# Expert gates applied to the tokens instead of to the expert outputs, in a windowed-attention and mixture-of-experts block

## The chip, the cores and the metric

The kernel runs on one core of a Trainium2 chip. The core has five engines that run side by side, each with its own queue of instructions: TensorE (PE in the profile; its weight loads are listed as PEld), VectorE (DVE), ScalarE (ACT), GpSimd (POOL) and SyncE (SP), which here only starts transfers. An engine works through its queue in order; where an instruction needs a result of another engine it waits, and what is queued behind it waits too. TensorE writes its results to PSUM, which this kernel uses as eight banks of 128 x 512 float32; the other operands lie in SBUF. The metric is the time of one execution on the device in microseconds, the median of several runs; the profile is of one execution.

## What is computed

The input x is 2 x 128 x 256 x 256 (batch, channels, rows, columns), float32. One layer follows: a channel normalisation and attention in windows of 8 x 8 pixels with a fixed mask that leaves only every second row and column, and on top of the sum with x a second normalisation and eight experts, of which each pixel takes the two best.

```python
x = x + _L0_conv_ref(_ln_c(x), W_qkv, W_out, rel_height, rel_width)   # window attention
t = _to_tokens(x)                                                     # one token per pixel, 128 channels
t = t + _L0_ffn_ref(_ln_t(t), router_w, router_b, expert_w, expert_b)
x = _from_tokens(t, x)

def _L0_ffn_ref(x, router_w, router_b, expert_w, expert_b):
    router_probs = jax.nn.softmax(x @ router_w + router_b, axis=-1)
    top_p, top_i = jax.lax.top_k(router_probs, K)                     # K = 2 of E = 8
    top_p = top_p / jnp.sum(top_p, axis=-1, keepdims=True)
    expert_out = jnp.einsum('bnd,edc->bnec', x, expert_w) + expert_b
    gathered = jnp.take_along_axis(expert_out, top_i[..., None], axis=2)
    return jnp.einsum('bnk,bnkc->bnc', top_p, gathered)
```

For each pixel the layer is thus the sum over the experts of gate times (normalised token times expert matrix, plus bias), where six of the eight gates are zero.

## The kernel before

**Tiling.** The image is cut into 64 strips of eight rows (32 for each batch element). A strip is one tile `xt` of 128 channels x 8 x 256, 1 MB, of which six fit (`xpool`). Because the mask couples only pixels of the same parity of row and column, the attention of a strip is done in four planes, n = 4i + pl, each of 4 x 128 = 512 pixels. The main loop runs over the 256 planes and six more steps that drain what is left. In a step n = 4i + pl four things are under way: the attention of plane n (`scores`, `attend`, `out_project`), the projection of the plane after it (`project`), the router for two rows (512 tokens) of the strip before (`norms`, `route`, with f = (i-1, pl)), and the experts for the rows routed one step earlier (`experts`). The same step also normalises two rows of the next strip for the attention (`norms` with c, then `ln1_c`).

**Normalisation.** `stats` transposes 512 tokens on PE (L211, tiles `px_f` and `px_c`) so that a token's channels lie along a row, and DVE takes their statistics (L213). `rstd` makes 1/std from them in ten small steps (L222 to L231). The means need no subtracting, since the weights were centred beforehand. `ln1_c` needs 1/std of each pixel on all 128 channel partitions: PE transposes a broadcast of it (L262, tile `pb`) and DVE multiplies (L265) into `xn`.

**Attention.** `project` makes q (L279, copied by ACT at L281), the relative position terms (`pu`, L288, followed by DVE's L290, L295 twice and L300), the keys (`pk`, L312, copied by ACT at L319), POOL's gather of the columns (L305) and the values (`pvv`, L329, copied at L336). `scores` adds up the scores in PSUM by many small matmuls (L357 and 128 of L372, two records each) and takes the exponential on ACT (L380). `attend` multiplies with the values (L391, L399), and DVE divides (L409 to L418). `out_project` multiplies with the output matrix (L424) and DVE adds into `xt` (L428).

**Router.** `norms` multiplies the tokens with the router matrix (L444, tile `plt`; copied by ACT at L452). `route` transposes the logits back to tokens on partitions (L466, `plg`), and a chain of DVE steps with one exponential on ACT (L470 to L496) finds the two best and leaves the gates in `gate` and the gates times 1/std in `gx`, with tokens on partitions.

**Experts.** `experts` transposes the gates (L505, `pg`) for a bias matmul (L511, `pbias`, copied to `acc` at L514). Then, for each 128 tokens, two matmuls of 128 x 512 (L520) apply four experts each, with the tokens as the stationary operand, so that the results have tokens on partitions and a gate is one number for each partition. DVE takes four experts from PSUM, multiplies by the gate and adds to `acc` (L531); ACT multiplies the other four by theirs (L535) into `others`, which POOL adds up (L536, L539, L540). At the end PE transposes `acc` back to channels (L544, `py`) and DVE adds it into `xt` (L545). After the fourth pair of rows the strip is stored (L552). `experts` is a generator: the main loop calls it in pieces with `next(parts)`, and finishes it as `behind` in the step after.

**Order.** The framework's scheduler sets the order on each engine, with the program's order as priority and a model of durations: what is ready earlier in its model can be put ahead of what is written earlier. It also makes the semaphores. PSUM has four rotating banks for matmul results (`ps_mm`) and four for the attention scores (`ps_att`). SP carries only the 1 MB loads (L98) and stores (L552) of the strips once the program has begun.

Of the kernel before, what the change touches and what calls it, by code (L numbers as in the profile page):

```python
# [16 lines left out]
P = 128  # L17
HEADS, DH = 4, 32
E = 8
SCALE = DH ** -0.5  # L20
CONV_EPS, FFN_EPS = 1e-6, 1e-5
NEG = -1e30

# [19 lines left out]
def kernel(  # L43
# [33 lines left out]
    ps_mm = ctx.enter_context(tc.tile_pool(name="ps_mm", bufs=4, space=PSUM))  # L77
# [72 lines left out]

    eb = ctile([NT * E, NT, P], "eb")
    nc.vector.memset(eb, 0.0)
    for t in range(NT):
        nc.scalar.dma_start(eb[t * E : (t + 1) * E, t, :], expert_b)
# [60 lines left out]
    def rstd(st, eps, n, name):  # L215

        u = small.tile([P, 2 * NT], F32, tag="u", name=f"u_{name}")[:, 0:n]
        d = small.tile([P, 2 * NT], F32, tag="d", name=f"d_{name}")[:, 0:n]  # L220
        r = small.tile([P, 2 * NT], F32, tag="r", name=f"r_{name}", bufs=6)[:, 0:n]
# [9 lines left out]
        nc.vector.scalar_tensor_tensor(r, u, 3.0, r, ALU.add, ALU.mult)  # L231
        return r
# [25 lines left out]
    def ln1_c(i, k, rs):  # L258

        pb = mm_tile(f"pb{i}_{k}")  # L260
        for t in range(NT):
            nc.tensor.transpose(  # L262
                pb[:, t * P : (t + 1) * P], rs[:, t : t + 1].broadcast_to([P, P]), ident
            )
        nc.vector.tensor_tensor(  # L265
            xn[i % 2][:, :, :, k, 1 : PC + 1],
            ln1_src(i, k).rearrange("p (y j x) -> p y x j", y=2, x=2),
            pb.rearrange("p (y j x) -> p y x j", y=2, x=2),
            ALU.mult,
        )  # L270

    def project(n, state):
# [12 lines left out]


        pu = mm_tile(f"pu{n}")
        nc.tensor.matmul(pu, lhsT=wrel, rhs=inner, start=True, stop=True)  # L288
        uT = work.tile([P, PR, 4, 32], F32, tag="uT", name=f"uT{n}")
        nc.vector.transpose(uT, pu.rearrange("p (a m s) -> p a s m", a=PR, s=4))  # L290
        for j in range(2):
            shifted = uT[:, :, :, NU * j + 3 : NU * j + 9]
            dims = [list(d) for d in shifted.ap]
            dims[1 + j][0] -= 1
            nc.vector.tensor_copy(  # L295
                auT[n % 2][:, :, :, 6 * j : 6 * j + 6],
                bass.AP(shifted.tensor, shifted.offset, dims),
            )
        au = work.tile([P, 2 * NP, PR, 4], F32, tag="au", name=f"au{n}")
        nc.vector.transpose(au.rearrange("p m a s -> p a s m"), auT[n % 2])  # L300
# [23 lines left out]

        vv = work.tile([P, HP, P], F32, tag="vv", name=f"vv{n}")
# [11 lines left out]
        state.update(qs=qs, kk=kk, au=au, vv=vv)  # L337
        yield
# [8 lines left out]
    def scores(n, state):  # L347

# [17 lines left out]
        for t in range(HP):  # L366
            for half in range(2):
# [13 lines left out]
        state.update(att=att, pT=pT)  # L381

# [47 lines left out]
    def norms(f, c, nm):  # L430


        st = small.tile([P, 2 * NT, 6], F32, tag="st", name=f"st{nm}", bufs=4)
        n0, n1 = (0 if f else NT), (2 * NT if c else NT)
        lT = None
# [17 lines left out]
        if not (f or c):  # L453
            return None, None, None
        r = rstd(st[:, n0:], epsc[:, n0:n1], n1 - n0, nm)
        return (r[:, 0:NT] if f else None), (r[:, NT - n0 :] if c else None), lT
# [4 lines left out]
    def route(i, k, rs, lT):  # L461
# [32 lines left out]
        nc.vector.tensor_tensor(gate, gate, sm.broadcast_to(by_e), ALU.mult)  # L494
        gx = small.tile([P, NT, E], F32, tag="gx", name=f"gx{nm}")
        nc.vector.tensor_tensor(gx, gate, rs.broadcast_to(by_e), ALU.mult)  # L496
        return gate, gx

    def experts(i, k, gate, gx):


        nm = f"{i}_{k}"
        src = rows_of(i, k)
        pg = mm_tile(f"pg{nm}")
        nc.tensor.transpose(pg[: NT * E, :P], gate.rearrange("p t e -> p (t e)"), ident)  # L505
        gT = small.tile([NT * E, P], F32, tag="gT", name=f"gT{nm}")
        nc.scalar.copy(gT, pg[: NT * E, :P])
        yield
        acc = work.tile([P, NT, P], F32, tag="acc", name=f"acc{nm}")
        pb = mm_tile(f"pbias{nm}")  # L510
        nc.tensor.matmul(  # L511
            pb, lhsT=gT, rhs=eb.rearrange("r t c -> r (t c)"), start=True, stop=True
        )
        nc.scalar.copy(acc.rearrange("p t c -> p (t c)"), pb)  # L514
        yield
        for t in range(NT):
            others = work.tile([P, 4, P], F32, tag="others", name=f"others{nm}_{t}")
            for e0 in range(0, E, 4):
                pe = mm_tile(f"pe{nm}_{t}_{e0}")
                nc.tensor.matmul(  # L520
                    pe,
                    lhsT=src[:, t * P : (t + 1) * P],
                    rhs=ew[:, e0 : e0 + 4, :].rearrange("p e c -> p (e c)"),
                    start=True,
                    stop=True,
                )
                for e in range(e0, e0 + 4):
                    pe_e = pe[:, (e - e0) * P : (e - e0 + 1) * P]
                    g = gx[:, t, e : e + 1]
                    if e < 4:  # L530
                        nc.vector.scalar_tensor_tensor(  # L531
                            acc[:, t, :], pe_e, g, acc[:, t, :], ALU.mult, ALU.add
                        )
                    else:
                        nc.scalar.activation(others[:, e - 4, :], pe_e, AF.Copy, scale=g)  # L535
            nc.gpsimd.tensor_tensor(  # L536
                others[:, 0:2, :], others[:, 0:2, :], others[:, 2:4, :], ALU.add
            )
            nc.gpsimd.tensor_tensor(acc[:, t, :], acc[:, t, :], others[:, 0, :], ALU.add)  # L539
            nc.gpsimd.tensor_tensor(acc[:, t, :], acc[:, t, :], others[:, 1, :], ALU.add)  # L540
            yield
        py = mm_tile(f"py{nm}")
        for t in range(NT):
            nc.tensor.transpose(py[:, t * P : (t + 1) * P], acc[:, t, :], ident)  # L544
        nc.vector.tensor_add(src, py, src)  # L545
        if k == R // 2 - 1:
            store(i)
        yield
# [6 lines left out]

    halo(0)
    for k in ln_rows(0):
        ln1_c(0, k, norms(None, (0, k), f"_{k}")[1])
    n_planes = 4 * len(strips)
# [4 lines left out]
    parts, behind = none, none  # L564
    for n in range(n_planes + 6):
        i, pl = divmod(n, 4)
        live = n < n_planes
        if pl == 0:
            load_x(i + 3)
            if i + 1 < len(strips):  # L570
                halo(i + 1)
        next(parts, None)
        if live:
            scores(n, states[n])
        f = (i - 1, pl) if 0 < i <= len(strips) else None
        rows = list(ln_rows(i + 1))[-4:] if i + 1 < len(strips) else []
        ks = [k for k in rows if (k - 2) % 4 == pl or (k == 1 and pl == 0)]
        if i + 1 < len(strips) and strips[i + 1][1] == 0:
            ks = list(ln_rows(i + 1))[pl::4]
# [83 lines left out]
```

## Time and profile before

| | |
|---|---|
| three runs | 5860.81 us median, 5839.03 to 5871.58 |
| the profiled execution | 5851.49 us, of which the span from its first to its last instruction is 5849.7 us |
| granted TensorE clock over the span | 0.974 |
| L531, DVE | 4096 instructions, 1394.6 us, 340 ns each |
| L535, ACT | 4096 instructions, 1199.5 us, 369 ns each |
| L536, L539, L540, POOL | 1024 each, 758.3, 479.0 and 468.1 us |
| L520, PE | 4096 records, two for a matmul; 184.0 us of idle time before them, put down to L535 |
| loads and stores | 64 each of 1024 KB, 4.8 and 5.2 us from issue to landing |
| HBM traffic | 23 GB/s over the span |

A group's line in the profile names its source line, engine and operation, the tile written and the tiles read, the shape, and how many there were; then come busy time, mean duration, and the time for which the engine sat idle just before, with what ended it. In an order of time the first figure is the start in us from the beginning of the span, the second the duration; a bracket gives idle time before the instruction and what released it. Durations of matmuls include their way through the array, so that consecutive ones overlap: the time that a matmul takes away from TensorE is read from start to start. A float32 matmul leaves two records.

### The profile page before, as it was taken

How to read it: one execution, taken by the hardware profiler on the slowest of the kernel's cores; microseconds unless marked ns; L12 is line 12 of the kernel's file. 1: busy time of each engine (PE TensorE's matmuls, PEld its weight loads, DVE VectorE, ACT ScalarE, POOL GpSimd, SP SyncE). 2: the span in 40 equal slices, each digit the busy share in tenths (PEclk: the TensorE clock that was granted, in tenths of full speed). 3: DMA queues.
4: the chain of work that ended last, by engine and by line, in shares of the span. 5: the costliest groups of instructions: out<-in, count | busy, mean ns of one | idle time of the engine just before them, and what ended most of it. 6: DMA issues, size and time to landing. Idle time of an engine off the chain costs nothing.

```text
span 5849.7 us, 221084 instructions
## 1 busy us (share of the span) xinstructions
PE 5470.1 (94%) x95758; PEld 3226.5 (55%) x95758; DVE 4262.2 (73%) x14184; ACT 2504.6 (43%) x7189; POOL 2057.8 (35%) x3667
## 2 busy tenths in 40 slices
PE   6999999999999999999999999999999999999998
PEld 4555555555555555555555555555555555555554
DVE  4767777767767777767767777767767767767766
ACT  2434444444444444444444444444444434434444
POOL 1333333333333333333333333333333333333334
PEclk8999999999999999999999999999999999999998
DMA  1000000000000000000000000000000000000000
GB/s 51 17 31 17 31 24 23 31 17 31 31 17 31 31 17 31 31 17 31 17 31 31 17 31 28 20 31 17 31 31 17 31 24 24 31 17 31 17 9 23
DMA packets 21957, 149.32 MB, mean 26 GB/s; under 512 B 2906, under 2 KB 4602, under 8 KB 4602
## 3 DMA queue, kind: packets, MB, share of 16 engines
q1 hardware_dynamic: 18432, 134.23, 6.1%
q8 instruction: 755, 12.37, 0.9%
q14 instruction: 216, 1.77, 0.1%
q10 hardware_dynamic: 2554, 0.95, 0.1%
HBM read 68.06 MB, written 67.11 MB: 23 GB/s over the span
## 4 chain that ended last, share of the span: by engine, by line
PE 83%; DVE 8%; ACT 6%; issue 2%; DMA 0%; ACTq 0%; POOL 0%; POOLq 0%; DVEq 0%
PE pe L520 32%; PE pvv L329 7%; PE att L372 6%; ACT others L535 6%; PE att L399 5%; PE pbias L511 5%; PE pk L312 4%; PE pq L279 3%; PE pu L288 3%; PE po L424 3%; PE att L357 3%; PE px_f L211 3%; PE att L391 3%; PE py L544 2%; PE px_c L211 2%
## 5 line engine op out<-in xcount | busy, mean ns | idle before, releaser
L520 PE MATMUL pe<-ew,xt 128*128 128x512 f32 x4096 | 2071.4, 629 | 184.0 <-ACT others L535 184.0
L535 ACT ACTIVATE others<-pe,gx 128x128 f32<-128x128 f32 x4096 | 1199.5, 369 | 1874.0 <-PE pe L520 1869.3
L536 POOL TENSOR_TENSOR others<-others 128x256 f32<-128x256 f32 x1024 | 758.3, 741 | 3324.8 <-ACT others L535 3226.3
L531 DVE SCALAR_TENSOR_TENSOR acc<-pe,gx,acc 128x128 f32<-128x128 f32 x4096 | 1394.6, 340 | 339.6 <-PE pe L520 301.3
L520 PEld LDWEIGHTS pe<-ew,xt 128*128 128x128 f32 x4096 | 725.8, 193 | 1123.1 <-issue 542.0
L213 DVE BATCH_NORM_STATS2 st<-px_f 128x6 f32<-128x128 f32 x1024 | 228.3, 286 | 959.8 <-PE px_f L211 959.8
L539 POOL TENSOR_TENSOR acc<-acc,others 128x128 f32<-128x128 f32 x1024 | 479.0, 468 | 262.8 <-DVE acc L531 207.1
L329 PEld LDWEIGHTS pvv<-wt,xcol 128*128 128x128 f32 x4096 | 476.9, 191 | 154.3 <-ACT others L535 114.6
L329 PE MATMUL pvv<-wt,xcol 128*128 128x128 f32 x4096 | 522.8, 281 | 1.7
L540 POOL TENSOR_TENSOR acc<-acc,others 128x128 f32<-128x128 f32 x1024 | 468.1, 457 | 75.6
L372 PE MATMUL att<-qs,kcol 32*64 32x32 f32 x32768 | 404.7, 225 | 68.5 <-issue 68.2
L380 ACT ACTIVATE pT<-att 128x1024 f32<-128x1024 f32 x256 | 262.3, 1025 | 445.1 <-PE att L372 445.1
L372 PEld LDWEIGHTS att<-qs,kcol 32*64 32x64 f32 x32768 | 396.0, 130 | 74.1 <-issue 73.5
L312 PE MATMUL pk<-xn,wt 128*128 128x390 f32 x1024 | 378.0, 491 | 0.0
L399 PEld LDWEIGHTS att<-pT,vv 64*32 64x32 f32 x32768 | 351.6, 105 | 47.5 <-issue 9.9
L336 ACT COPY vv<-pvv 128x512 f32<-128x512 f32 x512 | 300.8, 587 | 165.5 <-PE pvv L329 165.5
L399 PE MATMUL att<-pT,vv 64*32 64x32 f32 x32768 | 348.8, 201 | 5.5 <-issue 5.0
L305 POOL COPY xcol<-xn 128x480 f32<-128x480 f32 x512 | 302.1, 613 | 120.5 <-DVE xn L265 76.4
L511 PE MATMUL pbias<-eb,gT 32*128 32x512 f32 x512 | 311.7, 690 | 2.8 <-ACT lT L452 2.1
L312 PEld LDWEIGHTS pk<-xn,wt 128*128 128x128 f32 x1024 | 195.6, 191 | 194.9 <-issue 91.6
L424 PE MATMUL po<-o,wt 128*128 128x512 f32 x512 | 264.9, 599 | 12.8 <-DVE o L418 12.8
L300 DVE STREAM_TRANSPOSE au<-auT 128x512 f32<-128x512 f32 x256 | 270.5, 1057 | 0.2
(3777 smaller groups left out, 7019.7 us busy)
## 6 DMA issues: line engine op xcount, KB each, us to landing
xt<-in_x_dram SPq DMA_DIRECT2D x64, 1024.0 KB, 4.8
out_dram<-xt SPq DMA_DIRECT2D x64, 1024.0 KB, 5.2
ew<-in_L_ffn_expert_w_dram ACTq DMA_DIRECT2D x1, 512.0 KB
wall<-in_L_conv_W_qkv_dram ACTq DMA_DIRECT2D x1, 192.0 KB
keys<-in_c_keys_dram ACTq DMA_DIRECT2D x1, 64.0 KB, 7.5
wall<-in_L_conv_W_out_dram ACTq DMA_DIRECT2D x1, 64.0 KB
eb<-in_L_ffn_expert_b_dram ACTq DMA_DIRECT2D x4, 4.0 KB
ties<-in_c_ties_dram ACTq DMA_DIRECT2D x1, 32.0 KB
```

What stands on the lines that cost most here:

```text
L312: nc.tensor.matmul(pk[:, :nk], lhsT=wk, rhs=xp[:, r : r + 3, :].rearrange("p r c -> p (r c)"), start=True, stop=True,)
L329: nc.tensor.matmul(pv[:, t * P : (t + 1) * P], lhsT=xl[:, t0 + t].rearrange("p a k -> p (a k)"), rhs=wv, start=True, stop=True,)
L372: nc.tensor.matmul(sc[rows, h, 32 * t : 32 * t + 32], lhsT=kk[hp, half * HP + t, :], rhs=qs[hp, m0 : m0 + 2].rearrange("p m a s -> p (m a ...
L399: nc.tensor.matmul(av[hp, half, 32 * t : 32 * t + 32], lhsT=vv[rows, t, hp], rhs=pT[rows, h, 32 * t : 32 * t + 32], start=True, stop=True,)
L424: nc.tensor.matmul(po, lhsT=wo, rhs=state["o"].rearrange("p f z -> p (f z)"), start=True, stop=True)
L511: nc.tensor.matmul(pb, lhsT=gT, rhs=eb.rearrange("r t c -> r (t c)"), start=True, stop=True)
L520: nc.tensor.matmul(pe, lhsT=src[:, t * P : (t + 1) * P], rhs=ew[:, e0 : e0 + 4, :].rearrange("p e c -> p (e c)"), start=True, stop=True,)
L531: nc.vector.scalar_tensor_tensor(acc[:, t, :], pe_e, g, acc[:, t, :], ALU.mult, ALU.add)
L535: nc.scalar.activation(others[:, e - 4, :], pe_e, AF.Copy, scale=g)
L536: nc.gpsimd.tensor_tensor(others[:, 0:2, :], others[:, 0:2, :], others[:, 2:4, :], ALU.add)
L539: nc.gpsimd.tensor_tensor(acc[:, t, :], acc[:, t, :], others[:, 0, :], ALU.add)
L540: nc.gpsimd.tensor_tensor(acc[:, t, :], acc[:, t, :], others[:, 1, :], ALU.add)
```

## The change

The gates are applied to the tokens before the expert matmuls. `experts` now multiplies the 512 tokens, channels on partitions, by the gates of one expert (`xe`; every fourth expert on POOL, the others on DVE) and multiplies the product by that expert's matrix as the stationary operand. All eight, and a bias matmul over the eight rows of `ge`, sum in one PSUM bank of their own (`ps_acc`); DVE adds the bank into `xt`. The transposes `py` and the operations L531, L535, L536, L539, L540 and L514 are gone.

For this the gates must lie on all partitions. `route` writes the gates (g0) and the gates times 1/std (g1) into one tile `g`, into which `norms` writes the 1/std of the rows for the attention. `spread` transposes `g` on PE, copies it on ACT, writes it to DRAM, and reads it back with the last nine rows broadcast to all partitions (`gb`, 128 x 9 x 512) and the plain gates as eight rows (`ge`): three transfers on SP in each step. `ln1` takes 1/std from `gb` a step later and runs on POOL; `ln1_now` keeps the way over PE for rows that have no time for this. Rows for the attention are prepared two planes ahead (`rows_at`), and `halo` is called earlier for that.

The main loop is written anew, and within it PE keeps the written order, while the scheduler still orders the other engines. The scores are written in two parts with the q matmul between them; the `pu` group comes after the routing, and the values are made in two pieces after `out_project`. `ps_mm` has three banks for four.

```diff
-    ps_mm = ctx.enter_context(tc.tile_pool(name="ps_mm", bufs=4, space=PSUM))
+    gates = ctx.enter_context(tc.tile_pool(name="gates", bufs=2))
+    dram = ctx.enter_context(tc.tile_pool(name="dram", bufs=3, space=bass.MemoryType.DRAM))
+    ps_mm = ctx.enter_context(tc.tile_pool(name="ps_mm", bufs=3, space=PSUM))
+    ps_acc = ctx.enter_context(tc.tile_pool(name="ps_acc", bufs=1, space=PSUM))
...
+    def ln1(i, k, rb, eng):
+
+        eng.tensor_tensor(
+            xn[i % 2][:, :, :, k, 1 : PC + 1],
+            ln1_src(i, k).rearrange("p (y j x) -> p y x j", y=2, x=2),
+            rb.rearrange("p (y j x) -> p y x j", y=2, x=2),
+            ALU.mult,
+        )
...
         for t in range(HP):
+            if t == HP // 2:
+                yield
             for half in range(2):
...
+        g0, g1 = (
+            g[:, j * NT * E : (j + 1) * NT * E].rearrange("p (e t) -> p t e", t=NT)
+            for j in range(2)
+        )
+        nc.vector.tensor_tensor(g0, gate, sm.broadcast_to(by_e), ALU.mult)
+        nc.vector.tensor_tensor(g1, g0, rs.broadcast_to(by_e), ALU.mult)
+
+    def spread(f, c, g, nm):
+
+
+        lo, hi = (0 if f else 2 * NT * E), (2 * NT * E + NT if c else 2 * NT * E)
+        pg = mm_tile(f"pg{nm}")
+        nc.tensor.transpose(pg[: hi - lo, :P], g[:, lo:hi], ident)
+        gT = small.tile([(2 * E + 1) * NT, P], F32, tag="gT", name=f"gT{nm}")
+        nc.scalar.copy(gT[: hi - lo], pg[: hi - lo, :P])
+        gd = dram.tile([(2 * E + 1) * NT, P], F32, tag="gd", name=f"gd{nm}")
+        nc.sync.dma_start(gd[lo:hi], gT[: hi - lo])
+        gb = gates.tile([P, E + 1, NT * P], F32, tag="gb", name=f"gb{nm}")
+        lo = max(lo, NT * E)
+        nc.sync.dma_start(
+            gb[:, (lo - NT * E) // NT : (hi - NT * E) // NT].rearrange("p e k -> p (e k)"),
+            gd[lo:hi].rearrange("r k -> (r k)").partition_broadcast(P),
+        )
+        ge = None
+        if f:
+            ge = small.tile([E, NT * P], F32, tag="ge", name=f"ge{nm}")
+            nc.sync.dma_start(ge, gd[0 : NT * E].rearrange("(e t) k -> e (t k)", t=NT))
+        return gb, ge
+
+    def experts(i, k, gb, ge):
...
+        acc = ps_acc.tile([P, NT * P], F32, tag="acc", name=f"acc{nm}")
+        for e in range(E):
+            xe = work.tile([P, NT * P], F32, tag="xe", name=f"xe{nm}_{e}", bufs=4)
+            eng = nc.gpsimd if e % 4 == 3 else nc.vector
+            eng.tensor_tensor(xe, src, gb[:, e], ALU.mult)
+            nc.tensor.matmul(acc, lhsT=ew[:, e, :], rhs=xe, start=(e == 0), stop=False)
             yield
-        py = mm_tile(f"py{nm}")
-        for t in range(NT):
-            nc.tensor.transpose(py[:, t * P : (t + 1) * P], acc[:, t, :], ident)
-        nc.vector.tensor_add(src, py, src)
+        nc.tensor.matmul(acc, lhsT=eb, rhs=ge, start=False, stop=True)
+        nc.vector.tensor_add(src, acc, src)
         if k == R // 2 - 1:
             store(i)
         yield
...
+    with tc.manual_schedule(engines={mybir.EngineType.PE}):
+        for n in range(n_planes + 6):
+            i, pl = divmod(n, 4)
+            live = n < n_planes
+            if pl == 0:
+                load_x(i + 3)
+            score = scores(n, states[n]) if live else none
+            ahead = none
+            if n + 1 < n_planes:
+                states[n + 1] = {}
+                ahead = project(n + 1, states[n + 1])
+            next(score, None)
+            next(ahead, None)
+            next(score, None)
+            next(ahead, None)
+            if pl == 3 and i + 2 < len(strips):
+                halo(i + 2)
+            next(parts, None)
+            f = (i - 1, pl) if 0 < i <= len(strips) else None
+            cs = rows_at(n)
+            c = cs[0] if cs else None
+            if f or c:
+                g, rs, lT = norms(f, c, f"_{n}")
+            if spreads and spreads[1]:
+                ln1(*spreads[1], spreads[2][0][:, E], nc.gpsimd)
+            next(parts, None)
+            if live:
+                attend(n, states[n])
+            for _ in parts:
+                pass
+            if f:
+                route(*f, g, rs, lT)
+            next(ahead, None)
+            if spreads and spreads[0]:
+                parts = experts(*spreads[0], *spreads[2])
+            next(parts, None)
+            for c1 in cs[1:]:
+                ln1_now(*c1)
+            next(parts, None)
+            spreads = (f, c, spread(f, c, g, f"_{n}")) if f or c else None
+            if live:
+                out_project(n, states.pop(n))
+            next(parts, None)
+            next(ahead, None)
+            next(parts, None)
+            next(ahead, None)
```

## The prediction

> **What bounds the kernel now.** I read the page's totals first, then the chain that ended last, then the instructions in order of time in one plane of the middle, then the stretches with their granted clock. The page:
>
> ```profile
> span 5849.7 us, 221084 instructions
> PE 5470.1 (94%) x95758; PEld 3226.5 (55%) x95758; DVE 4262.2 (73%) x14184; ACT 2504.6 (43%) x7189; POOL 2057.8 (35%) x3667
> PE 83%; DVE 8%; ACT 6%; issue 2%; DMA 0%; ACTq 0%; POOL 0%; POOLq 0%; DVEq 0%
> PE pe L520 32%; PE pvv L329 7%; PE att L372 6%; ACT others L535 6%; PE att L399 5%; PE pbias L511 5%; PE pk L312 4%; PE pq L279 3%; PE pu L288 3%; PE po L424 3%; PE att L357 3%; PE px_f L211 3%; PE att L391 3%; PE py L544 2%; PE px_c L211 2%
> ```
>
> TensorE sets the end, and the expert matmuls (L520) are a third of it. Lines of PE in order of time (start, duration) in one plane, n = 45:
>
> ```profile
> 1022.10 1.98 PE L520 MATMUL pe<-ew,xt 128*128 128x512 f32 x4
> 1024.03 0.60 PE L262 MATMUL pb<-ident,r__44_15104 128*128 128x128 f32 x4
> 1025.38 1.98 PE L520 MATMUL pe<-ew,xt 128*128 128x512 f32 x4 [0.75 <-ACT others L535]
> 1027.20 1.02 PE L424 MATMUL po<-o,wt 128*128 128x512 f32 x2
> 1028.06 1.02 PE L279 MATMUL pq<-xn,wt 128*128 128x512 f32 x2
> 1038.37 1.12 PE L511 MATMUL pbias<-eb,gT 32*128 32x512 f32 x2
> 1041.24 0.60 PE L544 MATMUL py<-ident,acc 128*128 128x128 f32 x4
> 1043.49 1.12 PE L520 MATMUL pe<-ew,xt 128*128 128x512 f32 x2
> ```
>
> From 1022.10 to the same matmul at 1043.49 a plane takes 21.39 us, of which PE idles 0.75, waiting for ScalarE's L535. A 512-wide matmul occupies PE 0.86 us (po to pq; two records). From start to start the plane is: pe 7.17 in four groups, plg 0.11, pb 0.60, idle 0.75, po 0.86, pq 0.86, pu 0.87, pk 1.46, pvv 1.88, pg 0.21, scores 0.48 and 1.46, px_f 0.49, px_c 0.53, plt 0.36, pbias 1.05, py 0.53, attend 0.46 and 1.26: 21.39.
>
> **What PE loses.** pb (0.60) and py (0.53) go, and the idle 0.75 with L535. Eight expert matmuls stay 512 wide: 8 x 0.86 = 6.88 for 7.17; the bias one 0.86 for 1.05. The gate transpose stays (0.21). 21.39 - 0.60 - 0.53 - 0.75 - 0.29 - 0.19 = 19.03 us a plane. Some 254 planes' worth of FFN work (256, less the shorter ends): 254 x 2.36 = 600 us, a floor of 5250 if nothing new waits.
>
> **The other engines**, per plane (page busy / 256). DVE 16.65: less sixteen L531 (5.45) and L265 (0.68), plus six multiplications of 512 at the 0.68 of L265 and L428 (4.08) and one small operation more (0.16): 14.8. ACT 9.8: less sixteen L535 (4.69) and the L514 copy (0.59): 4.5. POOL 8.0: less L536, L539, L540 (6.66), plus two expert multiplications and the L265 one; 128 elements take 0.46 and 256 take 0.74, so 512 come to about 1.30 (estimate from these rows): 5.3. None passes PE. DMA: the broadcast writes 9 x 512 x 4 B x 128 = 2.36 MB a plane, 4.5 times today's 134 MB in all; the stretch 3028 to 3030 moved 389 GB/s, so 6.1 us of each plane. PSUM tiles fall from four to three: in the written order each is emptied at least two PE steps before its third successor wants it, so nothing; without that cover it would be one ScalarE copy, 0.59.
>
> Moves that cost nothing while their cover lasts: pu and its DVE group (0.70 + 0.38 + 1.06) go behind the routing, with 6.3 us of PE work before the next scores want au. pvv goes behind po, nine us ahead of attend. ln1 goes to POOL a plane later; rows are now made two planes ahead, and only xcol queues behind it.
>
> **New waits, and PE cannot step around them, since its order is fixed.** With scores at 0, by the durations above, PE ends the bias at 11.7, plg 11.8, pu 12.7, two expert matmuls 14.4, and then stands at the gate transpose (pg), behind which queue po, pvv and the next scores.
>
> (1) pg waits for the whole routing on DVE. Of DVE, the first and the last operations of the routing and what lies between them:
>
> ```profile
> 1025.24 0.18 DVE L470 TENSOR_TENSOR lg<-plg,r__44_15104 128x32 f32<-128x32 f32 x1
> 1025.63 0.55 DVE L471 TENSOR_TENSOR lg<-lg,rb 128x32 f32<-128x32 f32 x1
> 1026.10 0.68 DVE L265 TENSOR_TENSOR xn<-xt,pb 128x512 f32<-128x512 f32 x1
> ...
> 1031.39 0.34 DVE L531 SCALAR_TENSOR_TENSOR acc<-pe,gx,acc 128x128 f32<-128x128 f32 x1
> 1031.64 0.17 DVE L492 TENSOR_REDUCE sm<-gate 128x4 f32<-128x32 f32 x1
> 1031.74 0.20 DVE L295 COPY auT<-uT 128x96 f32<-128x96 f32 x1
> ...
> 1032.43 0.18 DVE L496 TENSOR_TENSOR gx<-gate,r__44_15104 128x32 f32<-128x32 f32 x1
> ```
>
> From plg's end (1024.19) to gx (1032.61) is 8.4 us today, because other operations lie between each two steps. The thirteen steps' own durations, each at its shortest, sum to 3.0. In the new order the residual addition (0.69) comes first: bias end 11.7 + 0.16 + 0.69 = 12.55, so pg is ready at 15.6 at best, a stall of 1.2; at today's pace (12.0 + 8.4 = 20.4) it is 6.0. Of what lay between, eight L531 and L265, 3.4 us, are gone. I take the low end, 1.2, as the row nearest to a DVE that has lost 1.9 us of load. 254 x 1.2 = 305.
>
> (2) The first expert matmul waits for that addition, since there is one accumulator: ready at 12.6, wanted at 12.7; 0, at most the 0.7 of one more addition, and then it would only shift the wait at pg.
>
> (3) The gates come by three transfers on SP: out (about 34 KB), broadcast, ge. No row shows so small a transfer in mid-run. Bounds from the 1 MB rows (landing 3.9 to 7.4): the first one below 3.9 and not above 7.4, the broadcast 2.25 times as much, 8.8 to 16.7; with the ScalarE copy (0.25) 13 to 24 us after pg. Cover to the next plane's first multiplication is 17 to 18 us at a 20 us plane. I take the low end (389 GB/s is nearer to it): hidden. The Trainium skill (DMA: Bandwidth & Descriptors, the table of fixed cost) gives about 2 us for setup and completion of a transfer; with that the chain would be estimated at about 10 us, still hidden. No row here shows it.
>
> (4) DVE and POOL. L471 takes 0.13 at its shortest and 0.55 here, while L536 runs on POOL. The change puts six two-input multiplications on DVE and three on POOL. Bounds: 0, or 0.5 for each of the ten or so such steps between px_f and pg, 5; I take what today's rows carry, already in the busy times. The Trainium skill (SBUF — State Buffer, "Who interferes with whom") speaks against the change: a DVE instruction with two SBUF inputs and a GpSimd one that reads exclude each other for their whole length. By it a multiplication could wait out a POOL one whole; L471's row agrees in kind.
>
> (5) The clock. Stretches of 2 us, with PE's busy time first and the granted clock after POOL's:
>
> ```profile
> 3012.00:3014.00 2.00, 2.00 (x123) 1.79 (x123) 0.00 (x0) 1.09 (x3) 1.86 (x4) 1.00 0.00 0
> 3014.00:3016.00 2.00, 0.68 (x68) 0.57 (x54) 0.00 (x0) 1.02 (x1) 0.00 (x0) 0.98 0.03 8
> 3016.00:3018.00 2.00, 1.24 (x6) 1.25 (x7) 0.09 (x1) 0.00 (x0) 0.00 (x0) 0.50 0.00 0
> ```
>
> A PE gap of 2.08 us, an "issue" one in the midst of the scores, halved the clock for 10 us, while the 0.75 in every plane leaves it at 1.00. So the stall of 1.2 lies near the harmless row, one of 3 would not: the gaps of about 2.6 before po in the first four planes are followed by slow matmuls in three (1.43, 1.61 and 2.05 for 1.02), for some 3.4 us each, 1.3 us lost on average over the four:
>
> ```profile
> 82.51 1.02 PE L424 MATMUL po<-o,wt 128*128 128x512 f32 x2 [2.75 <-DVE o L418]
> 114.64 2.05 PE L424 MATMUL po<-o,wt 128*128 128x512 f32 x2 [2.58 <-DVE o L418]
> ```
>
> Price at 1.2: 0, with 1.3 as the upper end (330 us).
>
> On the other side, the "issue" gaps before L372 total 68 us, and the clock averages 0.98 over 75 to 5680 us, which is about 2% or 110 us. They fall into the run of 128 score matmuls, which now has pq in its middle. Bounds 0 to 178; I take half, -90, as nothing shows which.
>
> **Sum.** 5849.7 - 600 + 305 - 90 = 5465; with the 11 us by which the median (5860.81) lies above this execution's span, about 5480.
>
> **Rivals.** *Routing holds PE* (slower). If au's group and expert multiplications slip between the routing steps as L531 did, the chain is 4.0 (today's durations, with POOL beside) + 1.1 (uT and its two copies) = 5.1, the stall 12.55 + 5.1 - 14.4 = 3.3, and the clock takes 1.3: 19.03 + 4.6 = 23.6 a plane, 5850 + 254 x 2.2 - 90 = about 6320. It decides from stall plus clock of 2.4 us on. For it: today's strict alternation on DVE. Against: most of what alternated is gone.
>
> *Gates late* (slower, slightly). SP works in order, and the load behind each strip's store already waits for it (276 us over 58 times, 4.8 each); gates queued behind both would come some 5 us late once in four planes: 64 x (5 + 1.7) = 430, about 5900. Against: four to five us of slack. At the 24 us end every plane would lack 6.
>
> *DVE is the bound* (no change). 14.8 plus twenty small waits of 0.3 for POOL is 20.8 and with its own waits for PE 21.4: about 5850.
>
> *The change does not do what it says*: no, the sixteen L531 and L535 have no counterpart in the new text.
>
> **How the numbers follow.** Forecast 0.58, routing 0.26, gates 0.11, DVE 0.05. A measurement of this kernel tells about 0.5% (the three runs spread by 0.55%). Faster 0.58, same 0.05, slower 0.37. The likeliest case by itself spans 5200 (no stall beyond 0.3 and the issue gaps gone) to 5750 (stall 2.3). The range reaches up to the routing case, 5200 to 6350; its far end (6.0 and the clock, near 7000) is left out.
>
> **What would show it.** Right: PE starts of a plane 20 to 20.5 us apart, a wait of PE's pg for DVE's last gate operation near 1.2, clock at 0.98 or above, issue gaps in L372 shorter. Wrong: pg waiting over 2.4, half clock in most planes (mean below 0.9), the first expert multiplication waiting for the broadcast, or DVE over 90% busy.

## The result and the profile after

The changed kernel takes 7218.79 us (median of four runs, 7215.22 to 7236.09) for 5866.17 before: a ratio of 1.232, 95% interval 1.228 to 1.237. It is 23% slower. The forecast was 5480 with a range to 6350.

The page of the changed kernel: the span, the busy time of the engines, the granted clock in 40 slices (tenths), transfers, and the engines' shares of the chain that ended last.

```profile
span 7220.1 us, 206144 instructions
PE 5844.1 (81%) x93746; PEld 3227.9 (45%) x93746; DVE 3843.6 (53%) x11635; ACT 1282.5 (18%) x2845; POOL 1423.9 (20%) x1355
PEclk8889898989899898899888998888888889898998
q1 hardware_dynamic: 78528, 749.23, 28.5%
PE 45%; DVE 43%; issue 5%; DMA 5%; ACT 2%; POOL 0%; SPq 0%; ACTq 0%; DVEq 0%
```

Before, PE held 83% of the chain and was busy for 94% of the span. Now PE and DVE share the chain almost evenly, and neither is busy throughout: they wait for each other. PE is less busy as a share and yet busier in microseconds, because its clock is lower: the mean is 0.896 for 0.974, and the slices show 8 in many places where there was 9. The queue of loads and stores (q1) moved 749 MB for 134.

PE in order of time in one step, n = 107 (start, duration, and idle time with its releaser):

```profile
3003.36 1.12 PE L557 MATMUL acc<-ge,eb 8*128 8x512 f32 x2
3004.41 0.33 PE L489 MATMUL plg<-ident,lT 128*128 128x128 f32 x1
3004.57 1.02 PE L322 MATMUL pu<-xn,wrel 128*128 128x512 f32 x2
3005.77 1.98 PE L555 MATMUL acc<-xe,ew 128*128 128x512 f32 x4 [0.17 <-DVE xt L558]
3011.28 0.43 PE L529 MATMUL pg<-ident,g 128*68 128x128 f32 x1 [3.53 <-DVE g L522]
3011.51 1.92 PE L440 MATMUL po<-o,wt 128*128 128x512 f32 x2
3024.10 0.43 PE L387 MATMUL att<-qs,kcol 32*64 32x32 f32 x7 [2.43 <-issue]
```

PE stands 3.53 us before the gate transpose, and the next matmul, po, takes 1.92 us instead of 1.02: the clock has halved. DVE in the same step, from the residual addition to the last gate:

```profile
3005.03 0.68 DVE L558 TENSOR_TENSOR xt<-acc,xt 128x512 f32<-128x512 f32 x1
3005.63 0.18 DVE L493 TENSOR_TENSOR lg<-plg,rs 128x32 f32<-128x32 f32 x1
3005.73 0.71 DVE L324 STREAM_TRANSPOSE uT<-pu 128x512 f32<-128x512 f32 x1
...
3006.93 0.69 DVE L554 TENSOR_TENSOR xe<-xt,gb 128x512 f32<-128x512 f32 x1
...
3007.88 1.03 DVE L334 STREAM_TRANSPOSE au<-auT 128x512 f32<-128x512 f32 x1
3008.77 0.39 DVE L507 TENSOR_TENSOR cmp<-cmp,ties 128x256 f32<-128x256 f32 x1
3009.09 0.67 DVE L554 TENSOR_TENSOR xe<-xt,gb 128x512 f32<-128x512 f32 x1
...
3011.01 0.21 DVE L522 TENSOR_TENSOR g<-g,rs 128x32 f32<-128x32 f32 x1
```

The routing (L493 to L522) runs from plg's end at 3004.74 to 3011.22, 6.5 us, and between its steps lie uT, its two copies, au and two expert multiplications, as the expert additions lay there before. What PE waited for, in total us, times and the longest:

```profile
PE pg L529 <- DVE g L522: 873.8, 251, 7.5
PE acc L555 <- DVE xt L558: 202.2, 137, 4.8
PE att L387 <- issue: 133.5, 53, 4.2
```

The stretches of 2 us around that wait (behind the length of the stretch PE's busy time; behind POOL's busy time the granted clock, and behind that the share of the DMA engines and GB/s):

```profile
3006.00:3008.00 2.00, 1.75 (x4) 0.45 (x3) 2.00 (x9) 0.23 (x1) 0.00 (x0) 1.00 0.00 0
3008.00:3010.00 2.00, 0.00 (x0) 0.00 (x0) 2.00 (x4) 0.00 (x0) 0.00 (x0) 0.96 0.00 0
3010.00:3012.00 2.00, 0.71 (x2) 0.56 (x3) 1.06 (x6) 0.25 (x1) 0.00 (x0) 0.50 0.00 0
3014.00:3016.00 2.00, 2.00 (x8) 1.42 (x7) 0.84 (x2) 0.00 (x0) 0.00 (x0) 0.50 0.79 249
```

Where the time went can be read from two figures of each page: PE's idle time is the span less its busy time, and the half clock costs about (1 - clock) x span.

| | span | PE idle | clock | clock's cost | the rest |
|---|---|---|---|---|---|
| before | 5849.7 | 380 | 0.974 | 152 | 5318 |
| after | 7220.1 | 1376 | 0.896 | 751 | 5093 |

PE's idle time grew by 996 us and the clock's cost by 599. Its work fell, by 225 us in this table. Idle time at half clock is counted in both columns, so the rest is too low, above all for the kernel after: counted only where PE was busy, the half clock costs 137 and 638 us, and the work fell by 126.

### The profile page after: what moved, and what is told of

Its sections match the earlier page's. It is cut to its first block, busy times and chain, and to the rows that moved or that the text cites. A ratio compares the mean times of both kernels' runs of the same rounds, so it can differ in the third digit from the quotient of the medians.

```text
span 7220.1 us, 206144 instructions
## 1 busy us (share of the span) xinstructions
PE 5844.1 (81%) x93746; PEld 3227.9 (45%) x93746; DVE 3843.6 (53%) x11635; ACT 1282.5 (18%) x2845; POOL 1423.9 (20%) x1355
## 4 chain that ended last, share of the span: by engine, by line
PE 45%; DVE 43%; issue 5%; DMA 5%; ACT 2%; POOL 0%; SPq 0%; ACTq 0%; DVEq 0%
PE acc L555 14%; DVE xe L554 12%; PE pvv L341 7%; PE pk L306 5%; PE att L387 5%; PE po L440 5%; DVE st L216 5%; DMA gb<-gd 4%; PE pq L289 3%; DVE au L334 3%; DVE xt L558 2%; DVE sT L425 2%; DVE rT L429 2%; DVE uT L324 2%; PE att L370 2%
## 5 line engine op out<-in xcount | busy, mean ns | idle before, releaser
L555 PE MATMUL acc<-xe,ew 128*128 128x512 f32 x4096 | 2365.5, 684 | 244.4 <-DVE xt L558 202.2
L554 DVE TENSOR_TENSOR xe<-xt,gb 128x512 f32<-128x512 f32 x1536 | 1183.4, 771 | 1970.3 <-PE acc L555 1788.0
L554 POOL TENSOR_TENSOR xe<-xt,gb 128x512 f32<-128x512 f32 x512 | 676.3, 1321 | 4613.7 <-PE acc L555 4585.2
L555 PEld LDWEIGHTS acc<-xe,ew 128*128 128x128 f32 x4096 | 806.0, 217 | 1106.6 <-issue 594.6
L341 PEld LDWEIGHTS pvv<-wt,xcol 128*128 128x128 f32 x4096 | 655.9, 227 | 356.2 <-issue 348.3
L529 PE MATMUL pg<-ident,g 128*68 128x128 f32 (+2 forms) x260 | 101.9, 392 | 873.9 <-DVE g L522 873.8
L341 PE MATMUL pvv<-wt,xcol 128*128 128x128 f32 x4096 | 636.4, 307 | 0.0
L263 POOL TENSOR_TENSOR xn<-xt,gb 128x512 f32<-128x512 f32 x248 | 378.0, 1524 | 1005.2 <-DMA gb<-gd 993.6
L440 PE MATMUL po<-o,wt 128*128 128x512 f32 x512 | 447.1, 972 | 9.3 <-DVE o L434 9.3
L444 DVE TENSOR_TENSOR xt<-po,xt 128x512 f32<-128x512 f32 x256 | 177.1, 692 | 515.1 <-PE po L440 515.1
L313 ACT COPY kcol<-pk 128x480 f32<-128x480 f32 x512 | 285.7, 558 | 63.0 <-PE pk L306 55.7
```

Source lines behind the costliest of these rows:

```text
L263: eng.tensor_tensor(xn[i % 2][:, :, :, k, 1 : PC + 1], ln1_src(i, k).rearrange("p (y j x) -> p y x j", y=2, x=2), rb.rearrange("p (y j x) ...
L313: nc.scalar.copy(kk[:, :, r * KC : (r + 3) * KC].rearrange("p t (r c) -> p t r c", c=KC), windows(pk[:, :nk].rearrange("p (r c) -> p r c", ...
L341: nc.tensor.matmul(pv[:, t * P : (t + 1) * P], lhsT=xl[:, t0 + t].rearrange("p a k -> p (a k)"), rhs=wv, start=True, stop=True,)
L440: nc.tensor.matmul(po, lhsT=wo, rhs=state["o"].rearrange("p f z -> p (f z)"), start=True, stop=True)
L554: eng.tensor_tensor(xe, src, gb[:, e], ALU.mult)
L555: nc.tensor.matmul(acc, lhsT=ew[:, e, :], rhs=xe, start=(e == 0), stop=False)
```

## The experiments

**Four first runs.** Theory A: PE stands at the gate transpose, and standing halves its clock. Rival B: the broadcast traffic delays PE's instructions, and this halves the clock. The first run only moves one line to the end of the step:

```diff
-            spreads = (f, c, spread(f, c, g, f"_{n}")) if f or c else None
             if live:
                 out_project(n, states.pop(n))
...
             next(ahead, None)
+            spreads = (f, c, spread(f, c, g, f"_{n}")) if f or c else None
```

> The changed kernel with the gate transpose and its three transfers written at the end of the step, behind po, pvv and two expert matmuls (4.5 us of PE work more between the routing and the transpose). Theory A (PE stands 3.5 us a plane at the gate transpose, and the clock halves because of it): that wait falls under 0.5 us a plane, the mean clock rises from 0.896 to 0.96 or more, 5300 to 5900 us. Rival B (the broadcast traffic starves PE of instructions, and this halves the clock): clock stays under 0.92, time over 6700 us. Rival C (gates late): pg's wait goes, but the first expert multiplications wait for the broadcast by some 3 us a plane, 6300 to 6700 us.

Measured: 7231 us (two runs), ratio 1.236 [1.226, 1.246], clock 0.894. Theory A's figures did not come true. Rival B's did (clock under 0.92, over 6700 us), while the waits are of the kind that C names: the wait at the transpose fell to a third, and waits for the transfers and behind them took its place. So this run does not tell the three apart; the later ones do. Its chain that ended last, where transfers have 33% for 5% in the changed kernel, three lines of its waits, and DVE and PE in order of time:

```profile
DVE 37%; DMA 33%; PE 25%; issue 5%; ACT 1%; SPq 0%; ACTq 0%; DVEq 0%
PE acc L555 <- DVE xt L558: 700.8, 214, 5.8
DVE xe L554 <- DMA gb<-gd: 541.0, 244, 4.1
PE pg L529 <- DVE g L522: 300.1, 226, 2.5
```

```profile
2999.75 0.69 DVE L554 TENSOR_TENSOR xe<-xt,gb 128x512 f32<-128x512 f32 x1 [2.17 <-DMA gb<-gd]
3000.36 1.46 DVE L233 SCALAR_TENSOR_TENSOR u__107_32445<-u__107_32445,r__107_32447 128x8 f32<-128x8 f32 x1
...
3006.55 0.68 DVE L558 TENSOR_TENSOR xt<-acc,xt 128x512 f32<-128x512 f32 x1
...
3007.29 3.78 PE L555 MATMUL acc<-xe,ew 128*128 128x512 f32 x4 [4.46 <-DVE xt L558]
```

The transpose is later, so the gates are, and now DVE waits for them: the scheduler put an expert multiplication ahead of the normalisation (L233), and behind it, in DVE's order, stand the softmax, the residual addition and the routing. PE in turn stands 4.46 us, for that addition. This is a loop: routing, gate transpose, transfers, first multiplication, and through DVE's order the next routing. It explains why a shift by 4.5 us within the step gains nothing. Theory A had to be widened to it; that is still an argument here, and the run with one step more of distance (below) tests it.

The second run fills the wait with useless work:

```diff
+        if f:
+            pd = mm_tile(f"pd{nm}")
+            for _ in range(4):
+                nc.tensor.matmul(
+                    pd,
+                    lhsT=wo,
+                    rhs=ew[:, 0:4, :].rearrange("p e c -> p (e c)"),
+                    start=True,
+                    stop=True,
+                )
         pg = mm_tile(f"pg{nm}")
```

> The changed kernel with four 512-wide matmuls of no use (3.4 us at full clock) ahead of every gate transpose, so that PE is busy where it waited 3.5 us. Theory A, which puts about 750 us to the halved clock: clock 0.95 or more, and the time falls although PE does more, to 6350 to 6800 us. If the clock falls for another reason (B), it stays near 0.90 and the time is 7100 us or more; if only the wait counts and not the clock, 7200.

Measured: 7660 us (one run), clock 0.912. A miss, and by its figures again nearest to rival B. PE's wait at the transpose fell to 23 us, but the gates come later, DVE waits 1003 us for the transfers (182 in the changed kernel), and PE 657 us for the residual addition. With the loop in the way this run cannot say what the clock costs.

The third leaves PE's order to the framework, the fourth takes the split of the scores out:

```diff
-    with tc.manual_schedule(engines={mybir.EngineType.PE}):
+    if True:
```

> The changed kernel without the fixed order on PE: the framework's scheduler orders PE too. Theory A: it puts ready work ahead of the gate transpose, whose wait falls under 1 us a plane; under 6200 us. If the fixed order is not what costs (the routing chain would hold any order), over 6800 us.

```diff
-            if t == HP // 2:
-                yield
```

> The changed kernel with the scores in one piece again, pq behind them. Theory A: the split is a side matter, within 150 us of 7219; more issue gaps in the 128 matmuls, as before, would make it slower by up to 100. If the split were part of the loss, faster by over 150 us.

Measured: 6924 us (one run) without the fixed order, and 7344 us (two runs, ratio 1.255 [1.246, 1.264]) with the scores whole. So the fixed order accounts for about 300 us and not for the bulk: its list still has 488 us for the residual addition and 465 us at the transpose. And the split is no part of the loss; it gains some 125 us (7344 less 7219), and without it the "issue" gaps in the score matmuls are 183 us for 134.

**Breaking the loop.** One step more lies between routing and experts. The transpose of a step goes into the next one, and the experts of these rows run whole in the step after that. The main new lines of the loop:

```diff
+            parts = experts(*ready[0], *ready[2]) if ready and ready[0] else none
             next(score, None)
+            next(parts, None)
             next(ahead, None)
+            next(parts, None)
             next(score, None)
+            next(parts, None)
             next(ahead, None)
...
+            spreads = (*pend[:2], spread(*pend)) if pend else None
+            next(ahead, None)
...
+            if spreads and spreads[1]:
+                ln1(*spreads[1], spreads[2][0][:, E], nc.gpsimd)
+            ready = spreads
+            pend = (f, c, g, f"_{n}") if f or c else None
```

> The changed kernel with one step more between routing and experts: the gate transpose of a step is written into the next step, behind its pk, and the experts of these rows run in the step after that, all within one step; pu comes right behind the keys, ln1 at the end. Theory A (a loop of routing, gate transpose, transfers and DVE's order is longer than a step, so that wherever the transpose stands, PE or DVE waits for it): with 20 us of cover both waits fall under 0.5 us a plane, the clock is 0.95 or more, 5400 to 6000 us. Rival B (the broadcast traffic takes PE's instructions away and with that the clock): over 6700 us, clock under 0.92.

Measured: 5619 us (two runs), ratio to the kernel before 0.962 [0.957, 0.967], clock 0.976. The same work, the same engines and the same traffic, 1600 us less. Its page and its wait at the transpose:

```profile
span 5608.0 us, 206222 instructions
PE 5234.5 (93%) x93746; PEld 2993.6 (53%) x93746; DVE 4579.1 (82%) x11635; ACT 1281.7 (23%) x2845; POOL 1723.6 (31%) x1355
```

```profile
PE plt L462 <- DVE uT L324: 147.3, 111, 1.4
PE pg L529 <- DVE g L522: 17.1, 51, 0.4
```

The wait of 874 us is 17, and that for the residual addition has gone from the list. PE's idle time is 374 us (5608.0 - 5234.5), and the clock costs 135 (0.024 x 5608). The routing itself did not get shorter. In one step:

```profile
2999.54 0.47 PE L489 MATMUL plg<-ident,lT 128*128 128x128 f32 x1
3006.65 0.22 DVE L522 TENSOR_TENSOR g<-g,rs 128x32 f32<-128x32 f32 x1
3011.95 0.27 PE L529 MATMUL pg<-ident,g 128*68 128x128 f32 x1
```

From plg's end to the last gate it takes 6.9 us (6.5 in the step of the changed kernel), but the transpose comes 5 us after that, with no wait. So it is the distance that counts.

**The traffic.** Constant gates (0.125 everywhere, so that this kernel leaves the real gates out of its result) take the transfers away and leave the routing where it is. A broadcast that nothing reads puts as many bytes into the kernel before.

```diff
-        gd = dram.tile([(2 * E + 1) * NT, P], F32, tag="gd", name=f"gd{nm}")
-        nc.sync.dma_start(gd[lo:hi], gT[: hi - lo])
...
+        gb, ge = gbc, gec if f else None
```

> The changed kernel with constant gates and 1/std (0.125) on all partitions, made once: the three transfers of every step are left out, while routing, gate transpose and its copy stay where they are. Theory A: PE still waits for the transpose, some 3.4 us a plane, and the clock stays under 0.93: 6600 to 7200 us. Rival B: without the traffic the clock recovers to 0.95 or more, under 6300 us.

```diff
+        gb = gates.tile([P, E + 1, NT * P], F32, tag="gb", name=f"gb{n}")
+        nc.sync.dma_start(
+            gb.rearrange("p e k -> p (e k)"),
+            x[0, 0, 0:18, :].rearrange("r k -> (r k)").partition_broadcast(P),
+        )
```

> The kernel before with a broadcast of 2304 KB from DRAM to all partitions in every step, which nothing reads. Theory A: the traffic by itself costs little, 5850 to 6010 us. Rival B: issue gaps and half clock as in the changed kernel, over 6300 us.

Measured: 6867 us without transfers (one run, clock 0.918), with PE's wait at the transpose even longer:

```profile
PE pg L531 <- DVE g L524: 1133.8, 255, 8.0
PE att L389 <- issue: 10.8, 27, 0.7
```

No loop through transfers is left here, and PE still stands for the routing, 4.4 us a plane: the length of the routing alone makes that wait, and by the first run the transfers are what keeps a later transpose from curing it. The "issue" gaps, in contrast, nearly go, from 206 us in all in the changed kernel to 15.

The kernel before with the traffic takes 6103 us (two runs), ratio 1.045 [1.042, 1.048], clock 0.956: neither theory's figure, between the two. Two lines of its page (the clock and the DMA engines' busy share in 40 slices) and its "issue" gaps in the score matmuls and in attend:

```profile
PEclk8989989989998999999999999999999999989999
DMA  9576878786887600000000000000000000000000
PE att L373 <- issue: 119.4, 69, 4.3
PE att L400 <- issue: 64.6, 21, 5.1
```

Before they were 68.2 and 5.0. The traffic is not spread over the steps, as the edit has it: nothing waits for it, so SP issues the broadcasts one behind another at some 310 GB/s, and all are out at 2123 us. The changed kernel moves 104 GB/s over its span. All of the loss lies in that first third: from 75 to 2130 us the clock is 0.91, behind it 0.98, and the 30170 matmul records of that stretch take 2055 us, where 30253 take 1800 in the kernel before (75 to 1875). So these bytes, packed as they are, cost the kernel before some 250 us, by longer gaps in which PE has nothing to run and the clock that follows them; what they would cost spread over the steps this run does not say. It is a real cost, but rival B does not carry the result: without any of the traffic the changed kernel still takes 6867 us, and with all of it the two-step kernel is faster than the kernel before.

**The routing's length.** pu and with it DVE's au group behind the transpose:

```diff
-            next(ahead, None)
             if spreads and spreads[0]:
                 parts = experts(*spreads[0], *spreads[2])
...
             spreads = (f, c, spread(f, c, g, f"_{n}")) if f or c else None
+            next(ahead, None)
```

> The changed kernel with pu and with it DVE's au group (0.71 + 0.41 + 1.03 us) written behind the gate transpose, so that they no longer lie between the routing's steps; PE has 0.87 us less to do ahead of the transpose. Theory A: the wait at the transpose falls from 3.4 to some 2 to 2.5 us a plane and the time by 200 to 600 us, to 6600 to 7000. If the interleaving on DVE is not what makes the routing long, the wait grows by 0.9 and the time to 7400.

Measured: 7196 us (one run), clock 0.882. Half a hit: the wait is as expected, 606.5 / 251 = 2.4 us a plane, the time is not. In the step at 3000 us the routing takes 5.4 us from plg's end (3004.30 to 3009.71) for 6.5, and in the median of all steps 6.2 for 6.7. So the au group makes the routing longer, but by 0.5 to 1.1 of its 2.15 us; L494, L496 and L497 start 0.2 us apart in both kernels, with uT's copies between them in one and nothing in the other. And nothing is gained: PE has lost the pu matmul that covered the residual addition. The two waits below come to 1048 us together, in the changed kernel to 1076.

```profile
PE pg L529 <- DVE g L522: 606.5, 251, 10.2
PE acc L555 <- DVE xt L558: 441.2, 250, 5.9
```

**The clock by itself.** With constant gates no transfer can come late, so the useless matmuls can be tried again: the lines of the second run, with `range(5)`.

> The kernel with constant gates (no transfers) and five 512-wide matmuls of no use (4.3 us at full clock) ahead of every gate transpose, which there waits 4.4 us a plane. There are no transfers here that a later transpose could make late. If the standing PE is what halves the clock (it costs (1 - 0.918) x 6866 = 563 us there): clock 0.95 or more and 6400 to 6750 us, faster with more work. If the clock falls for another reason: 0.92 or less and 6850 to 7150 us.

Measured: 6697 us (two runs; 6867 without the added matmuls), clock 0.980 for 0.918. 1280 more matmuls, five in each of 256 steps, and the kernel is 170 us faster. The clock cost 563 us there and now 134 (0.020 x 6703). The wait that is left, and the clock in 40 slices:

```profile
PE pg L541 <- DVE g L524: 194.4, 62, 3.7
PEclk8999999999999999999999999999999999999999
```

The routing and its place are the same, only PE is busy where it stood. That the standing halves the clock is shown.

**On the two-step kernel.** Three changes of one place each: the scores whole (the edit of the fourth run); pu behind plt; the framework's order for PE (that of the third).

> The kernel with two steps between routing and experts, and the scores in one piece again (the first expert matmul and pq behind them). If the split helps by itself: slower by 20 to 150 us, 5640 to 5770, with more issue gaps in the score matmuls. If it is of no use: within 20 us of 5619.

> The kernel with two steps between routing and experts, and pu behind px_f, px_c and plt and one expert matmul, since plt waits there for the PSUM tile that DVE empties of pu (147 us over 111 times). Faster by 100 to 250 us, 5370 to 5520, if that wait is not replaced; 5560 to 5680 if another takes its place (au for the next scores).

```diff
             spreads = (*pend[:2], spread(*pend)) if pend else None
-            next(ahead, None)
...
             next(parts, None)
+            next(ahead, None)
             next(parts, None)
             if live:
                 attend(n, states[n])
```

> The kernel with two steps between routing and experts, and PE ordered by the framework's scheduler. If the distance between routing and experts is what counts and not who orders PE: 5450 to 5900 us. If the written order is needed besides: over 6000.

Measured: 5748 us with the scores whole (two runs, 0.983 [0.980, 0.986]); the split is worth 129 us, and the gaps before the score matmuls, absent from the list with it, are 151 us without. 5595 us with the framework's order (one run): once the distance is there, who orders PE hardly matters. With that order in both kernels, the distance takes the time from 6924 to 5595, so it is not the new places of PE's instructions within the step that gained it. And 5412 us with pu moved (four runs), 0.926 [0.923, 0.928] of the kernel before and the fastest of the study. Its page:

```profile
span 5411.8 us, 205959 instructions
PE 5204.4 (96%) x93746; PEld 2992.1 (55%) x93746; DVE 4665.6 (86%) x11635; ACT 1282.3 (24%) x2845; POOL 1779.7 (33%) x1355
PEclk8999999999999999999999999999999999999998
DVE 37%; PE 34%; DMA 27%; issue 2%; ACT 1%; SPq 0%; ACTq 0%; DVEq 0%
```

PE's idle time is 207 us and the clock is 0.990. The chain that ended last (the last line) still goes through DVE, PE and the transfers: PE is busy nearly throughout, and DVE still waits for the transfers, 219 us over 240 times.

## Why the prediction was wrong

- **The step that failed is (1), the wait of pg.** The prediction had both ends, 1.2 and 6.0 us, and took the low one because most of what lay between the routing's steps was gone. It was 3.48 us (873.8 / 251). In the step shown the residual addition ends 1.2 us after the bias matmul (0.85 in the prediction; DVE still had a multiplication of the attention ahead of it), and from there to the last gate it is 5.5 us, where the sum had the 3.0 of the routing's own steps. What was gone from between them was replaced by other ready work: the two expert multiplications in the step shown (1.36 us) besides the au group with its two copies (2.15), and the scheduler alternates as before. The rival "routing holds PE" had the place and the mechanism; the choice between the cases was wrong, not the list of them. That its 3.3 us is so near is partly luck: it counted 4.0 for the routing's own steps, which took 3.1, and left out the third operation of the au group (1.03) and the multiplications.
- **(5), the clock, failed with it.** It was priced at 0 for a stall of 1.2, and at most 330 us. It cost 599 us more than before, 2.4 us a plane, where the rival had 1.3. The price came from four gaps, three of them followed by some 3.4 us of half clock. Here 238 of the 251 waits have half clock in them or within 2 us behind them, 5.1 us of it in the mean. In the step shown a second gap, at the scores, halves it once more (2.43 us at 3024); such gaps come 53 times.
- **(2) was taken as 0 and is 202 us.** It has the same cause: the softmax and the multiplications stand ahead of the residual addition on DVE.
- **(3), the gates, was about right for this order and wrong as a margin.** In the step shown the broadcast is issued at 3013.79 and the first user starts at 3022.33, 8.5 us; the estimate was 8.8. The first transfer, bounded by 3.9 to 7.4 us, took 1.75 from its issue (3012.04) to that of the broadcast that waits for it, near the 2 us of the prediction's other figure. From the transpose to the first user it is 11 us, not 13 to 24. The gates were not hidden in every step: DVE stands for them 26 times, 182 us in all. And the slack of four to five us was the whole reserve of the loop. The first run used it up, and the transfers had 33% of its chain.
- **The issue gaps did not shrink.** -90 was taken; they are 206 us in all, where before they were 94. The split helps, by 125 and 129 us in two pairs of kernels, and the traffic, which the prediction did not connect with them, takes more: without it they are 15.
- **PE's work** fell by 126 to 225 us by the table above, for 410 expected (600 less the 190 of idle time in it). The term that was too small is "8 x 0.86": among other matmuls an expert matmul takes 0.95 to 0.96 from start to start (two take 1.92, 3001.44 to the bias matmul at 3003.36) and the bias one 1.05, not 0.86. In the kernel with pu moved a plane without any wait takes 19.82 us (pq at 3019.61 to pq at 3039.43), where the prediction had 19.03.
- **The sum.** From 5465 to the span of 7220 it is 1755 us: 569 at the transpose (874 for 305), 599 of clock, 202 at the residual addition, some 200 of issue gaps and some 185 of PE's work (by the table's 225). The rival's 6320 is 900 us too low for the same terms without the first: the clock above its 330, (2), the issue gaps and the work. The lower end of the likeliest case does not come out of its own terms either: 5250 + 76 - 178 + 11 is 5159, not 5200.
- **(4), DVE and POOL**, cost about what the rows said. A multiplication on DVE takes 0.63 at its shortest, 0.69 in the median, 0.77 in the mean and 2.04 at its longest (0.68 was taken), one on POOL 1.32 (1.30), and L471's counterpart 0.15 in the step shown. Where POOL's multiplication falls beside it, a small operation is long: L233 took 1.46 us in the lines of the first run and 0.17 a step later. That this did not decide is argued: DVE's busy time fell, to 53% of the span.
- **The floor came out, partly by luck.** 5250 and "20 to 20.5 us a plane" describe the kernel with pu moved and two steps between: 5412 us, 20.4 a plane in the median. PE's work there is some 240 us more than the floor had (5150 for 4908); the clock costs 54 us, where the floor kept the 152 of before. The change has a gain in it: 225 us with two steps between (5844 to 5619), 435 with pu moved besides (5848 to 5412). The distance of one step loses 1600.

## What to carry to other kernels

A fixed order on one engine is only as good as the longest chain on the others between two of its entries. Before fixing it, add up that chain with what the scheduler will put between its steps (take the pace that the trace shows, not the sum of the chain's own durations), and keep more independent work between than that. Where a wait moves from place to place without the time changing, look for a loop through several engines' queues: here no shift within the step helped, and one more step of distance did. And price a stall of PE with its clock, which here cost 599 us beside 996 of idle time.

## What the runs showed of the hardware

- Useless matmuls in place of a standing PE made a kernel faster: 6867 to 6697 us with 1280 more of them, clock 0.918 to 0.980. A wait of 0.75 us in every plane of the kernel before left the clock at 1.00: half clock begins at none of its 250 waits for L535.
- The "issue" gaps have a place. Count PE's instructions in the trace (matmuls, weight loads and the few semaphore ones) in blocks of 256: all 85 such gaps of 0.3 us or more in the kernel before, and all 117 in the changed one, come at the same place of a block, to within one instruction. So PE runs dry only where one block of 256 instructions ends and the next begins, in the kernel before 62 times of 85 in the runs of small attention matmuls. That it waits for the next block to be brought is what this suggests; it is not shown.
- Broadcasts of 2304 KB that nothing reads, issued one behind another at 310 GB/s, made the kernel before 4.5% slower, all of it in the 2100 us that they took: the gaps grew from 68 to 119 us in the scores and from 5 to 65 us in attend. The changed kernel without its transfers has 15 us of such gaps for 206.
- Splitting 128 small matmuls by one large one made two kernels faster by 125 and 129 us. That the large one gives the next instructions time to arrive is argued, not shown.
